# A transformer block's attention stage: the second head group's queries made between the first four heads, and the roots of the tiles' variances later in GpSimd's order

## The chip, the cores and the metric

The kernel runs on one core of a Trainium2 chip. The metric is the device time of one launch in microseconds; before the change it is 2590.26 us, the median of three runs (2590.1 to 2594.9).

The core has five engines with a queue each, which work through their queues in order: TensorE (PE in the profile; its weight loads are shown apart as PEld), VectorE (DVE), ScalarE (ACT), GpSimd (POOL) and SyncE (SP), which here only starts DMAs. GpSimd starts the gathers, DMAs whose rows are chosen by an index.

## The reference

Everything is fp32. `x` is 4 x 512 tokens of 512 features, `ctx` is 4 x 512 tokens of 256 features. Four branches are added to `x` one after the other, each on a layernorm of it:

```python
x = x + ssm(ctx, layernorm(x), ...)         # a selective scan
x = x + moe(layernorm(x), ...)              # 64 experts, 8 for each token, rerouted by similarity
x = x + attention(layernorm(x), ctx, ...)   # the stage that the change touches
x = x + ffn(layernorm(x), w1, w2)           # quantized, ternary weights

def attention(h, ctx, Wq, Wk, Wv, Wo, gq, gk):      # 16 heads of 128
    q = rmsnorm(h @ Wq, gq)                         # normed for each token and head
    k = rmsnorm(ctx @ Wk, gk)
    v = ctx @ Wv
    attn = softmax(q @ k.T / sqrt(128))             # for each batch and head, 512 x 512
    return (attn @ v) @ Wo
```

The layernorm in front needs, for each token, the mean and the variance of its 512 features and the variance's inverse root. The MoE branch ends with a weighted sum of eight rows for each token.

## The kernel before

The phases run one after the other: the scan, the routing, the experts, and then `attend` (L1808), which holds the attention and the FFN and takes about the second half of the time. In `attend` the order of instructions is the program's own: each engine's queue gets them in the order in which the Python code emits them, and no scheduler moves them.

Tokens come in tiles of 128: four tiles for each of four batches. Heads come in groups of four; a group is a batch with four heads, 16 groups in all, 64 heads. A head's work on one tile is a *unit*, so a head has four units and `u` counts them, 0 to 255.

The steps of a tile (batch 0 at the start, later batches while the batch before is at work):
- `fetch` (L1835): one gather by GpSimd of 128 rows of the experts' outputs (256 KB). Eight for each tile. They land in four buffers `yg` in turn, and in the first tiles in `yg_first` (four places) and `yg_more` (eight places) too.
- `add` (L1844): VectorE adds the weighted row to `x_all`.
- `stats` (L1850): on VectorE mean and variance (`bn_stats`, `bn_aggr`), and on GpSimd the addition of epsilon and the power -0.5 (L1857, L1859), which gives `rstd_c`.
- `normed` (L1862): VectorE makes `xn_c`, which waits for `rstd_c`.
- `turn_x` (L1868): four transposes on TensorE, and a copy to `xnT` by ScalarE.

The steps of the queries of a tile for a group:
- `queries` (L1910): four matmuls with 512 columns into `pq`; ScalarE squares them into `sq`.
- `norm_q` (L1921): VectorE sums the squares of each head (`qms`, L1924), GpSimd makes the inverse root `rq` (L1926, L1927).
- `scale_q` (L1930): VectorE multiplies, `qn`.
- `turn_q` (L1935): four transposes on TensorE into `pqt`, a copy to `qT` by ScalarE.

The steps of a unit: `scores` (L1945: a matmul, the maximum `mx` on VectorE, exp on ScalarE), `weights` (L1958, VectorE: reciprocal and scaling), `turn` (L1963: transposes `pet`, copy `eT` by ScalarE). Once a head, `values` (L1972) multiplies by v, after the last `eT` of its head is there. Once a head and group, `project` (L1980) multiplies by Wo for one tile of the group before.

Two parts of `attend` set the order:

*The first tiles.* A list of steps is made with `later(time, step)`, sorted by time (L2260), and emitted. The times have no effect but the order. It holds the 32 fetches and additions of batch 0 (L2191 to L2196), eight whole key tasks (`some_keys`: keys of later heads, `pk`, whose results SP stores to `k_dram`), and then for each of the four tiles one window (L2217 to L2239): `turn_x`, two more key tasks, the queries of groups 0 *and* 1, the scores of head 0 on this tile, and some of the weights and turns. Loads of Wq (1 MB each), of the keys, their norms and the values of head 0, 1 and 2 (`load_kv`) and the norming of those keys (`norm_k`, by VectorE here) have their times in the list too (L2240 to L2244). As SP works in order, a load whose turn has come behind a key's store starts when this store has been started.

*The loop over units* (L2270), from `u = 4` on: the scores of `u`, the values of the head before where `i == 2`, the turn of `u - 2`, then what `front[u]` holds (TensorE's extra work), the weights of `u - 1`, and what `back[u]` holds (work without TensorE). `front` and `back` are filled from L2101 on. For the groups 1 to 14 the loop makes the queries of the group behind: of each head `h` the tile `h`'s, at `u + 1` to `u + 4` (L2110 to L2115). In group 0's heads it makes none, as group 1's have been made between the first tiles. In the loop, keys are normed by GpSimd (L2123), and GpSimd fetches three rows of the next batch for each head (L2130).

Of the kernel before, what the change touches and what calls it, by code (L numbers as in the profile page):

```python
# [17 lines left out]
F32 = mybir.dt.float32  # L18
# [6 lines left out]
ALU = mybir.AluOpType  # L25
# [4 lines left out]
P = 128  # L30
B, S, DM = 4, 512, 512
NT = B * S // P
NC = DM // P
CTX = 256
EPS = 1e-5
DS, DC, DR = 16, 4, 16
NG = 4
E, TOPK, SEL, FI = 64, 8, 4, 192
# [692 lines left out]
def moe_phase(ctx, cm, x_all, w, kv, dr, router_stats, out):  # L731
# [33 lines left out]
    with tc.manual_schedule():  # L765
        attend(cm, x_all, w, kv, y_dram, r["wk"], r["pos"], tern, late, ctx_k, keys.wk, out)
# [386 lines left out]
class Keys:  # L1153
# [4 lines left out]
    KB = S // P  # L1158
# [649 lines left out]
def attend(ctx, cm, x_all, w, kv, y_dram, wk, pos, tern, late, ctx_k, wk_k, out):  # L1808
# [5 lines left out]
    tc, nc = cm.tc, cm.nc  # L1814
    pool = {n: ctx.enter_context(tc.tile_pool(name=f"c_p{n}", bufs=n)) for n in (1, 2, 3, 4, 7)}
    small = ctx.enter_context(tc.tile_pool(name="c_small", bufs=3))
# [5 lines left out]
    KB = S // P  # L1822
    NG4 = H // HG
    half = pool[1].tile([P, HG], F32, name="half")
    nc.vector.memset(half, -0.5)
    groups = [(b, g) for b in range(B) for g in range(NG4)]
    heads = [(b, g, h) for b, g in groups for h in range(HG)]
    xnTs, st = {}, {}
# [21 lines left out]
    def stats(t, name):  # L1850
# [8 lines left out]
        nc.gpsimd.tensor_tensor(rstd, ve, half[:, 0:1], ALU.pow)  # L1859
        st[name, t] = mv, rstd  # L1860

    def normed(t, name):  # L1862
        mv, rstd = st.pop((name, t))
        xn = st[name, t] = pool[1].tile([P, DM], F32, name=f"xn_{name}")
        nc.vector.tensor_scalar(xn, x_all[:, t, :], mv[:, 0:1], rstd, ALU.subtract, ALU.mult)
        return xn
# [154 lines left out]
    def ffn_x(t):  # L2021
        xn = normed(t, "d")
        mx = small.tile([P, 1], F32, name="mxa")
        nc.vector.tensor_reduce(mx, xn, AX.X, ALU.max, apply_absolute_value=True)
        ff[t] = scales(mx, tern.mean[0], "a")
# [75 lines left out]
    front, back = {}, {}  # L2101

    def put(where, u, f, *a):
        where.setdefault(u, []).append((f, *a))

    last = len(groups) - 1
    for n, (b, g, h) in enumerate(heads):
        j = n // HG
        u = n * KB
        if j < last and j > 0:  # L2110
            after = groups[j + 1]
            put(front, u + 1, queries, *after, h)
            put(back, u + 2, norm_q, *after)
            put(back, u + 3, scale_q, *after)
            put(front, u + 4, turn_q, *after, h)  # L2115
        if j > 0:
            put(front, u + 4, project, j - 1, h)
            put(back, u + 5, take_projected, j - 1, h)
        if h == 0:
            put(back, u, load_q, j + 2)  # L2120
            put(back, u + 1, load_o, b, g)
        put(back, u + 3, load_kv, n + 3)
        put(back, u + 3, norm_k, n + 2)  # L2123
        at = n % H
        if b + 1 < B:
            for k in range(3):
                if 0 <= 3 * (at - 2) + k < NC * TOPK:
                    put(back, u + k, add, 1)
            if 0 <= 3 * (at - 1) < NC * TOPK:
                put(back, u + 2, fetch, min(3, NC * TOPK - 3 * (at - 1)))  # L2130
            if at >= 11 and at < 15:
                t = (b + 1) * NC + at - 11
                put(back, u + 1, stats, t, "c")
                put(back, u + 3, normed, t, "c")
                put(front, u + 4, turn_x, t)
        if b > 0 and h == 1:
            t = (b - 1) * NC + g
            put(back, u + 2, stats, t, "d")
            put(back, u + 4, ffn_x, t)
            put(back, u + 5, ffn_xq, t)  # L2140
            put(front, u + 6, ffn_xT, t)

            put(front, u + 7, ffn_up, t, 0)
            put(front, u + 11, ffn_up, t, 1)
            for k, at in enumerate((8, 9, 12, 12)):
                put(back, u + at, ffn_max, t, k)
            put(back, u + 12, ffn_h, t)
            for k in range(4):
                put(back, u + 13 + k // 2, ffn_hq, t, k)
            put(front, u + 14, ffn_hT, t, 0)  # L2150
            put(front, u + 15, ffn_hT, t, 1)
            put(front, u + 15, ffn_down, t, 0)
            put(front, u + 19, ffn_down, t, 1)
            put(back, u + 20, ffn_y, t)
            put(back, u + 21, store, t)
# [26 lines left out]
    def later(time, f, *a):  # L2182
        steps.append((time, len(steps), f, a))

    START, GAP, FLIGHT = 3.0, 1.35, 6.0
    FRONT, WINDOW = 21.0, 14.5

    wide = [pool[1].tile([P, KB, S], F32, name="yg_first", tag="eT")]
    wide += [pool[2].tile([P, HG, DM], F32, name="yg_more", tag="Wo") for _ in range(2)]
    places = [t[:, k] for t in wide for k in range(KB)]  # L2190
    for n in range(NC * TOPK):  # L2191
        at = n % 16 - KB
        if n >= 16 and 0 <= at < KB:
            at = -1
        later(START + n * GAP, fetch, 1, places[at] if at >= 0 else None)
        later(START + n * GAP + FLIGHT, add, 1)  # L2196

    left = list(KEYS_LATE)

# [13 lines left out]

    for i in range(H // 2):
        later(2.6 * i, some_keys)
    later(FRONT + 0.4, key_ends)
    for i in range(NC):  # L2217
        end = START + ((i + 1) * TOPK - 1) * GAP + FLIGHT
        later(end + 0.1, stats, i, "c")
        later(end + 2.3, normed, i, "c")  # L2220
        at = FRONT + i * WINDOW
        later(at, turn_x, i)
        later(at + 0.5, key_task)
        later(at + 2.2, queries, 0, 0, i)
        later(at + 5.6, key_ends)
        later(at + 6.4, norm_q, 0, 0)
        later(at + 6.5, queries, 0, 1, i)
        later(at + 8.5, scale_q, 0, 0)
        later(at + 10, turn_q, 0, 0, i)
        later(at + 10.4, key_task)  # L2230
        later(at + 10.8, norm_q, 0, 1)
        later(at + 12.1, scores, 0, i)
        later(at + 12.9, scale_q, 0, 1)
        later(at + 13, key_ends)
        later(at + 14, turn_q, 0, 1, i)
        if i < KB - 1:
            later(at + 14.7, weights, 0, i)
        if i < KB - 2:
            later(at + 15, turn, 0, i)  # L2239
    for f, n, time in ((load_q, 0, 9.5), (load_kv, 0, 14.5), (load_q, 1, 17.5), (load_kv, 1, 44),  # L2240
                       (load_kv, 2, 50)):
        later(time, f, n)
    for n in range(3):
        later(FRONT + (0, 2.5, 3.2)[n] * WINDOW + 9, norm_k, n, nc.vector)  # L2244

    def last_norms():
        rsqrt(nc, small, ms, ms, "late")
# [22 lines left out]
    for u in range(KB, len(heads) * KB + 2):  # L2270
        n, i = divmod(u, KB)
# [30 lines left out]
    for i in range(NC + 1):  # L2302
        t = t0 + i
# [103 lines left out]
```

## Time and profile before

| | us |
|---|---|
| median of three runs | 2590.26 |
| the profiled execution, its own time | 2586.95 |
| its span in the trace | 2585.2 |
| TensorE busy | 2444.9 (95%) |
| VectorE busy | 1497.1 (58%) |
| ScalarE busy | 1210.4 (47%) |
| GpSimd busy | 1179.4 (46%) |
| granted TensorE clock, mean | 0.978 |

Stages of the trace, by TensorE's instructions:

| stage | from | to | TensorE busy, share | clock |
|---|---|---|---|---|
| scan, routing, experts | 0 | 1339.0 | 1239.28, 93% | 0.97 |
| eight key tasks, first gathers | 1339.0 | 1363.2 | 22.30, 92% | 0.91 |
| windows of the four first tiles | 1363.2 | 1436.1 | 66.83, 92% | 0.91 |
| units 4 to 16 | 1436.1 | 1468.6 | 28.92, 89% | 1.00 |
| units 17 to the last head | 1468.6 | 2506.0 | 1024.84, 99% | 1.00 |
| last tiles' FFN | 2506.0 | 2585.0 | 62.68, 79% | 0.98 |

How to read it: times count from the start of the span. In a line of the trace stand the start, the duration, the engine, the line of the program, the operation with its output and inputs, how many were merged, and in brackets how long the engine had stood idle before it and what released it. A PE row's duration ends when its last result is there; the next row can start before this, so the pace is read from start to start. The clock is the share of TensorE's full speed that was granted; 0.5 is half speed. An engine that is idle costs time only where something that sets the end waits for it.

### The profile page before, as it was taken

How to read it: one execution, taken by the hardware profiler on the slowest of the kernel's cores; microseconds unless marked ns; L12 is line 12 of the kernel's file. 1: busy time of each engine (PE TensorE's matmuls, PEld its weight loads, DVE VectorE, ACT ScalarE, POOL GpSimd, SP SyncE). 2: the span in 40 equal slices, each digit the busy share in tenths (PEclk: the TensorE clock that was granted, in tenths of full speed). 3: DMA queues.
4: the chain of work that ended last, by engine and by line, in shares of the span. 5: the costliest groups of instructions: out<-in, count | busy, mean ns of one | idle time of the engine just before them, and what ended most of it. 6: DMA issues, size and time to landing. Idle time of an engine off the chain costs nothing. (4 is left out here: it accounts for less than half of the span.)

```text
span 2585.2 us, 29327 instructions
## 1 busy us (share of the span) xinstructions
PE 2444.9 (95%) x9781; PEld 1377.1 (53%) x9831; DVE 1497.1 (58%) x2565; ACT 1210.4 (47%) x2323; POOL 1179.4 (46%) x1105
## 2 busy tenths in 40 slices
PE   6989889987999999999998999999999999999997
PEld 3555555645556566667664444445455554554543
DVE  6999998945322443344225565456655666555446
ACT  6777777654232222233323543454454454544543
POOL 7999999923333444444425333134322343121112
PEclk8999999988999999999998999999999999999999
DMA  5362535244666677899756543233433453332210
GB/s 203 95 224 88 202 126 190 101 141 166 197 211 215 215 227 251 278 336 336 251 172 196 182 122 112 82 112 109 132 104 100 138 143 102 96 95 64 62 48 21
DMA packets 228013, 403.60 MB, mean 156 GB/s; under 512 B 62211, under 2 KB 103235, under 8 KB 223760
## 3 DMA queue, kind: packets, MB, share of 16 engines
q1 hardware_dynamic: 184798, 246.71, 29.4%
q0 software_dynamic: 41008, 154.76, 19.2%
q8 instruction: 81, 1.33, 0.2%
q10 hardware_dynamic: 2050, 0.18, 0.1%
q14 instruction: 76, 0.62, 0.1%
HBM read 313.88 MB, written 79.82 MB: 152 GB/s over the span
## 5 line engine op out<-in xcount | busy, mean ns | idle before, releaser
L1952 DVE TENSOR_REDUCE mx<-psc 128x1 f32<-128x512 f32 x256 | 176.6, 690 | 403.1 <-PE psc L1949 402.9
L1282 PE MATMUL pg<-xT,wg 128*128 128x284 f32 (+12 forms) x1536 | 394.2, 400 | 1.8 <-ACT xT L1269 1.1
L1955 ACT ACTIVATE e<-psc,mx 128x512 f32<-128x512 f32 x256 | 176.1, 688 | 325.2 <-DVE mx L1952 324.6
L1282 PEld LDWEIGHTS pg<-xT,wg 128*128 128x128 f32 x1536 | 279.0, 192 | 85.4 <-issue 36.5
L492 POOL TENSOR_TENSOR dBu<-bb,du 128x1024 f32<-128x1024 f32 x128 | 304.6, 2400 | 4.0 <-DVE dA L517 2.8
L1223 POOL DMA_INDIRECT xg<-xn_dram,tok x168 | 173.9, 1035 | 198.7 <-PE pt L1266 156.3
L1949 PE MATMUL psc<-kT,qT 128*128 128x512 f32 x512 | 261.7, 593 | 0.0
L1976 PE MATMUL po<-eT,v 128*128 128x512 f32 x512 | 231.4, 595 | 8.5 <-ACT eT L1970 8.3
L1915 PE MATMUL pq<-Wq,xnT 128*128 128x512 f32 x512 | 231.7, 595 | 0.0
L1985 PE MATMUL px<-Wo,oT 128*128 128x512 f32 x512 | 231.5, 595 | 0.0
L1969 PEld LDWEIGHTS pet<-ident,e 128*128 128x128 f32 x1024 | 126.3, 141 | 147.3 <-issue 129.0
L1926 POOL TENSOR_SCALAR qms<-qms 128x4 f32<-128x4 f32 x64 | 24.9, 389 | 390.5 <-DVE qms L1924 389.6
L503 ACT ACTIVATE dA<-delta,negA 128x512 f32<-128x512 f32 x256 | 176.5, 695 | 49.3 <-DVE hc L518 27.1
L517 DVE TENSOR_TENSOR_SCAN dA<-dA,dBu 128x1024 f32<-128x1024 f32 x80 | 185.4, 2318 | 14.9 <-ACT dA L503 5.2
L1327 DVE COPY yo<-po 128x512 f32<-128x512 f32 x68 | 47.0, 691 | 217.4 <-PE po L1316 217.4
L1976 PEld LDWEIGHTS po<-eT,v 128*128 128x128 f32 x512 | 96.1, 190 | 134.7 <-issue 114.6
L1969 PE MATMUL pet<-ident,e 128*128 128x128 f32 x1024 | 154.8, 274 | 7.0 <-DVE e L1961 6.8
L523 PEld LDWEIGHTS yT<-ident,hc 128*128 128x128 f32 x1024 | 119.1, 144 | 78.7 <-issue 36.1
L1961 DVE TENSOR_SCALAR e<-e,tot 128x512 f32<-128x512 f32 x256 | 155.0, 605 | 9.1
L523 PE MATMUL yT<-ident,hc 128*128 128x128 f32 x1024 | 133.1, 278 | 20.5 <-POOL hc L518 9.0
L1223 POOL DMA_INDIRECT wd<-down,widx x64 | 62.8, 981 | 194.0 <-PE po L1316 181.6
L1970 ACT COPY eT<-pet 128x512 f32<-128x512 f32 x256 | 148.2, 579 | 3.4 <-PE pet L1969 2.9
(358 smaller groups left out, 4276.4 us busy)
## 6 DMA issues: line engine op xcount, KB each, us to landing
y_dram<-yo SPq DMA_DIRECT2D x110, 256.0 KB
bb<-bc_dram SPq DMA_DIRECT2D x16, 1024.0 KB
cb<-bc_dram SPq DMA_DIRECT2D x16, 1024.0 KB
v_dram<-v SPq DMA_DIRECT2D x64, 256.0 KB
k_dram<-k_kT SPq DMA_DIRECT2D x64, 256.0 KB
Wq<-Wq SPq DMA_DIRECT2D x16, 1024.0 KB
kT<-k_dram SPq DMA_DIRECT2D x64, 256.0 KB
rk<-r_dram SPq DMA_DIRECT2D x64, 256.0 KB
```

The source lines that it names most:

```text
L492: nc.gpsimd.tensor_tensor(dBus[q], st[b]["bb"][i // 2][:, j:j + 2, :], st[b]["du"][c].unsqueeze(1).to_broadcast([P, 2, S]), ALU.mult)
L503: nc.scalar.activation(dAs[q][:, j, :], st[b]["delta"][c], AF.Exp, scale=negA[:, c, n:n + 1])
L517: nc.vector.tensor_tensor_scan(*flat, 0.0, ALU.mult, ALU.add)
L523: nc.tensor.matmul(yT[:, lc, :], t[:, lc * P:(lc + 1) * P], cm.ident, is_transpose=True, start=first and lc == 0, stop=last, skip_group_ch ...
L1223: nc.gpsimd.indirect_dma_start(out=t[0:n, :], out_offset=None, in_=table, in_offset=bass.IndirectOffsetOnAxis(ap=index, axis=0))
L1282: nc.tensor.matmul(pg[:, 0:n], s["wg"][:, c, m * P:(m + 1) * P], s["xT"][:, c, 0:n], start=c == 0, stop=c == NC - 1)
L1915: nc.tensor.matmul(pq.rearrange("p h d -> p (h d)"), xnTs[b * NC + i][:, c, :], s["Wq"][:, c, :], start=c == 0, stop=c == NC - 1)
L1949: nc.tensor.matmul(pscore, st[b, g]["qT"][:, h, i * P:(i + 1) * P], ks[n], start=True, stop=True)
L1952: nc.vector.tensor_reduce(mx, pscore, AX.X, ALU.max, negate=True)
L1969: nc.tensor.transpose(pt[:, kc, :], e[:, kc * P:(kc + 1) * P], cm.ident)
L1976: nc.tensor.matmul(po, v[:, kc, :], eT[:, kc, :], start=kc == 0, stop=kc == KB - 1)
L1985: nc.tensor.matmul(px, oTs[j * HG + h][:, i * P:(i + 1) * P], st[b, g]["Wo"][:, h, :], start=h == 0, stop=h == HG - 1)
```

## The change

The queries of group 1 leave the windows of the first tiles. They go into the loop, to the units of the first four heads: of head `h` the queries at unit 4 + 3h, the sums and roots one unit later, the scaling two, the turn three units later.

In the first tiles, `stats` is split for them: `stats_c` has the VectorE part, `root_c` the two GpSimd instructions, which are put 2.2 later in the list, so behind more fetches in GpSimd's order.

The times of the list are set anew: a fetch every 1.27, from the 15th on every 1.56, additions 5.5 instead of 6.0 behind; the windows start at 20.6, 32, 44 and 56.5 instead of every 14.5 from 21 on. In a window the second key task stands where the second group's queries stood, the scores at 11.9 instead of 12.1. The loads move: the first Wq from 9.5 to 13.6, head 0's keys from 14.5 to 18.2, the second Wq from 17.5 to 45, heads 1 and 2's keys from 44 and 50 to 50 and 56.

```diff
+    def stats_c(t):
+        sts = small.tile([P, 6], F32, name="st_c")
+        nc.vector.bn_stats(sts, x_all[:, t, :])
+        mv = small.tile([P, 2], F32, name="mv_c")
+        nc.vector.bn_aggr(mv, sts)
+        st["c", t] = mv
+
+    def root_c(t):
+        mv = st["c", t]
+        ve = small.tile([P, 1], F32, name="ve_c")
+        nc.gpsimd.tensor_scalar(ve, mv[:, 1:2], EPS, None, ALU.add)
+        rstd = small.tile([P, 1], F32, name="rstd_c")
+        nc.gpsimd.tensor_tensor(rstd, ve, half[:, 0:1], ALU.pow)
+        st["c", t] = mv, rstd
...
-        if j < last and j > 0:
+        if j == 0:
+            at, after = KB + 3 * h, groups[1]
+            put(front, at, queries, *after, h)
+            put(back, at + 1, norm_q, *after)
+            put(back, at + 2, scale_q, *after)
+            put(front, at + 3, turn_q, *after, h)
+        elif j < last:
...
-    START, GAP, FLIGHT = 3.0, 1.35, 6.0
-    FRONT, WINDOW = 21.0, 14.5
+    FETCH = [3.4 + 1.27 * n + 0.29 * max(0, n - 14) for n in range(NC * TOPK)]
+    FLIGHT = 5.5
+    FRONT = (20.6, 32, 44, 56.5)
...
-        later(START + n * GAP, fetch, 1, places[at] if at >= 0 else None)
-        later(START + n * GAP + FLIGHT, add, 1)
+        later(FETCH[n], fetch, 1, places[at] if at >= 0 else None)
+        later(FETCH[n] + FLIGHT, add, 1)
...
-        end = START + ((i + 1) * TOPK - 1) * GAP + FLIGHT
-        later(end + 0.1, stats, i, "c")
+        end = FETCH[(i + 1) * TOPK - 1] + FLIGHT + 0.1
+        later(end, stats_c, i)
+        later(end + 2.2, root_c, i)
         later(end + 2.3, normed, i, "c")
-        at = FRONT + i * WINDOW
+        at = FRONT[i]
         later(at, turn_x, i)
         later(at + 0.5, key_task)
         later(at + 2.2, queries, 0, 0, i)
         later(at + 5.6, key_ends)
         later(at + 6.4, norm_q, 0, 0)
-        later(at + 6.5, queries, 0, 1, i)
+        later(at + 6.5, key_task)
         later(at + 8.5, scale_q, 0, 0)
-        later(at + 10, turn_q, 0, 0, i)
-        later(at + 10.4, key_task)
-        later(at + 10.8, norm_q, 0, 1)
-        later(at + 12.1, scores, 0, i)
-        later(at + 12.9, scale_q, 0, 1)
-        later(at + 13, key_ends)
-        later(at + 14, turn_q, 0, 1, i)
+        later(at + 8.9, key_ends)
+        later(at + 9.8, turn_q, 0, 0, i)
+        later(at + 11.9, scores, 0, i)
         if i < KB - 1:
-            later(at + 14.7, weights, 0, i)
+            later(at + 15.5, weights, 0, i)
         if i < KB - 2:
-            later(at + 15, turn, 0, i)
-    for f, n, time in ((load_q, 0, 9.5), (load_kv, 0, 14.5), (load_q, 1, 17.5), (load_kv, 1, 44),
-                       (load_kv, 2, 50)):
+            later(at + 16, turn, 0, i)
+    for f, n, time in ((load_q, 0, 13.6), (load_kv, 0, 18.2), (load_q, 1, 45), (load_kv, 1, 50),
+                       (load_kv, 2, 56)):
         later(time, f, n)
```

On GpSimd the order of the first tiles becomes: fetches 0 to 13, the root of tile 0, fetches 14 to 17, `norm_q` of tile 0, fetches 18 to 20, the root of tile 1, fetches 21 to 25, `norm_q` of tile 1, fetches 26 to 28, the root of tile 2, fetches 29 to 31, `norm_q` of tile 2, the root of tile 3, `norm_q` of tile 3. Before, it was: fetches 0 to 11, the root of tile 0, fetches 12 to 18, `norm_q` of tile 0 for group 0, fetch 19, the root of tile 1, fetches 20 and 21, `norm_q` for group 1, fetches 22 to 27, the root of tile 2, and so on.

More of the change, by code (lines that the diff above doesn't have):

```diff
@@ L2215, in attend @@
         later(2.6 * i, some_keys)
-    later(FRONT + 0.4, key_ends)
+    later(FRONT[0] + 0.45, key_ends)
     for i in range(NC):
-        end = START + ((i + 1) * TOPK - 1) * GAP + FLIGHT
-        later(end + 0.1, stats, i, "c")
+        end = FETCH[(i + 1) * TOPK - 1] + FLIGHT + 0.1
+        later(end, stats_c, i)
+        later(end + 2.2, root_c, i)
         later(end + 2.3, normed, i, "c")
-        at = FRONT + i * WINDOW
+        at = FRONT[i]
         later(at, turn_x, i)
@@ L2226, in attend @@
         later(at + 6.4, norm_q, 0, 0)
-        later(at + 6.5, queries, 0, 1, i)
+        later(at + 6.5, key_task)
         later(at + 8.5, scale_q, 0, 0)
-        later(at + 10, turn_q, 0, 0, i)
-        later(at + 10.4, key_task)
-        later(at + 10.8, norm_q, 0, 1)
-        later(at + 12.1, scores, 0, i)
-        later(at + 12.9, scale_q, 0, 1)
-        later(at + 13, key_ends)
-        later(at + 14, turn_q, 0, 1, i)
+        later(at + 8.9, key_ends)
+        later(at + 9.8, turn_q, 0, 0, i)
+        later(at + 11.9, scores, 0, i)
         if i < KB - 1:
-            later(at + 14.7, weights, 0, i)
+            later(at + 15.5, weights, 0, i)
         if i < KB - 2:
-            later(at + 15, turn, 0, i)
-    for f, n, time in ((load_q, 0, 9.5), (load_kv, 0, 14.5), (load_q, 1, 17.5), (load_kv, 1, 44),
-                       (load_kv, 2, 50)):
+            later(at + 16, turn, 0, i)
+    for f, n, time in ((load_q, 0, 13.6), (load_kv, 0, 18.2), (load_q, 1, 45), (load_kv, 1, 50),
+                       (load_kv, 2, 56)):
         later(time, f, n)
-    for n in range(3):
-        later(FRONT + (0, 2.5, 3.2)[n] * WINDOW + 9, norm_k, n, nc.vector)
+    for n, time in enumerate((29, 62, 66)):
+        later(time, norm_k, n, nc.vector)
     def last_norms():
```

## The prediction

> **What bounds the kernel.** I read the engines' shares first, then the granted clock and the engines' busy time stage by stage, then TensorE in order of time through the stretch that the change touches. TensorE (PE) carries the kernel: 2444.9 of 2585.2 us, and it makes 42% of the chain of waits against 3% for the next engine. But the share hides stages. The busy times of TensorE, cut at turn_x of the tiles 0 to 3 (1363.2, 1385.8, 1403.6, 1421.2), at the loop's first score (1436.1) and at its unit 17 (1468.6), are these (columns: stretch, its length, busy and instructions, clock, DMA share, GB/s):
>
> ```profile
> 1363.20:1385.80 22.60, 19.38 (x62) 0.82 0.67 230
> 1385.80:1403.60 17.80, 16.20 (x61) 0.94 0.73 216
> 1403.60:1421.20 17.60, 16.85 (x61) 0.90 0.25 81
> 1421.20:1436.10 14.90, 14.40 (x56) 1.00 0.09 33
> 1436.10:1468.60 32.50, 28.92 (x104) 1.00 0.69 217
> ```
>
> The last window, nothing waiting and the clock full, takes 14.9 us; the first three take 22.6, 17.8 and 17.6. So the first tiles hold 13.3 us of waits and half clock, the first four heads about 5. Nothing else in the kernel is touched, so the gain has to come from these. TensorE's own rows show where it goes:
>
> ```profile
> 1384.93 1.12 PE L1942 MATMUL pqt<-ident,qn 128*128 128x128 f32 x4 [3.06 <-DVE qn L1933]
> ...
> 1403.10 0.66 PE L1942 MATMUL pqt<-ident,qn 128*128 128x128 f32 x4 [1.50 <-DVE qn L1933]
> 1403.59 0.60 PE L1872 MATMUL pt<-ident,xn_c 128*128 128x128 f32 x4
> 1404.44 0.69 PE L1969 MATMUL pet<-ident,e 128*128 128x128 f32 x4 [0.25 <-ACT qT L1943]
> 1404.92 3.58 PE L1182 MATMUL pk<-k_ctx,k_w 128*128 128x512 f32 x4
> ...
> 1421.59 1.88 PE L1182 MATMUL pk<-k_ctx,k_w 128*128 128x512 f32 x4
> 1423.31 3.60 PE L1915 MATMUL pq<-Wq,xnT 128*128 128x512 f32 x8
> ```
>
> The reader is to see that a wait is paid twice: the pause itself (3.06, 1.50), and the same four key matmuls at 3.58 instead of 1.88 us behind it.
>
> **What moves out of the first tiles.** Start to start, at full clock: queries 3.43 us (1423.31 to 1426.74), its four turns 0.44. The second group's four of each leave: 4 x 3.87 = 15.5 us of TensorE. Their squares, sums, roots, scalings and copies leave with them; those lay beside TensorE. Of SP's queue, the second Wq (1 MB) goes from 1359.8 to behind the third tile's first key store, the first Wq behind two more key stores (1352.2 to about 1357), head 0's key and value loads behind the eighth store (1357.0 to about 1362). I cost these at nothing: the first Wq still has 10 us before its first use, where the trace shows 2.5 MB (Wq, Wo, a key, its norms) landing in the 12 us from 1435.0 to 1447.3. If that cover fails, the first window ends 2 to 3 us later. Below nothing is possible too: gathered rows land in 7.5 us beside the two Wq's and in 3.2 to 5.6 without.
>
> **What this leaves on the path.** Less TensorE work saves only where TensorE sets the pace, and after the change the windows are set by a ring of static orders. In GpSimd's new order the root of tile 1 stands behind norm_q of tile 0 and three fetches; that norm_q stands behind tile 0's queries. So from turn_x to turn_x, in rows of the trace:
>
> - Tile 0. Fetch 11 starts at 1356.94; two more at 1.26 end at 1360.4; the root takes 0.24 + 0.97, xn_c 0.6: turn_x at 1362.4 against 1363.20. In GpSimd's old order it stalled 3.38 us for this root; the new place removes that, as meant, but what it frees is fetches, not the end.
> - Window 0. turn_x to the end of queries as now (1363.20 to 1373.27) 10.1; end of queries to end of the root rq 3.0 (2.8 at 1426.91 to 1429.69, 3.7 in the first window); fetches 18 to 20 at 1.3 each 3.9; root 1.1 and xn_c 0.6: 18.7, so turn_x(1) at 1381.1 (now 1385.84). TensorE idles from about 1376.5.
> - Window 1. turn_x 0.44, score 0.86, keys 1.72, queries 3.60, and 3.0 more because 4.6 us of pause leave the first three at half clock: 9.6. Then 2.9 + 3.9 + 1.7: 18.1, turn_x(2) at 1399.2 (now 1403.59).
> - Window 2. 5.8 + 2.2 for half clock; rq 2.8; scaling 0.7, the last addition 0.7, statistics 0.9 (DVE's order has them behind the scaling); 1.7: 14.8, turn_x(3) at 1414.0 (now 1421.15).
> - Window 3. 5.8 + 1.1 (half of the half-clock price); rq 2.8, scaling 0.7, turns with their copy 1.3, score 0.9: 12.6, the loop at 1426.6 (now 1436.12).
>
> So the first tiles give back 9.5 us, not 15.5.
>
> The half clock is where a rule is weighed. The Trainium skill, TensorE: Matmul & The Clock Gate, section HAM oscillation, puts the danger at PE idle gaps over about 3.4 us; it speaks against this change, which turns a full TensorE into one with pauses of 4.6 and 3.9 us. The rows above are stricter: half clock behind 3.06 and behind 1.50 + 0.25. By the rule window 3 (pause 2.4) is at full clock, by the rows it pays 2.2; I took 1.1. Windows 1 and 2 pay by both.
>
> **What the heads pay.** Units 4 to 16 now take 32.5 us for 13 x 1.30 (score 0.86, turn 0.44) + 3 x 3.43 (values) = 27.2 us of work; 5.3 are waits, like this one:
>
> ```profile
> 1449.48 1.02 PE L1949 MATMUL psc<-kT,qT 128*128 128x512 f32 x2
> 1451.47 3.70 PE L1976 MATMUL po<-eT,v 128*128 128x512 f32 x8 [0.97 <-ACT eT L1970]
> ```
>
> Added are the 15.5 us. Could they fall into the 5.3? Only where they stand between a score and what waits for it. Queries go to units 4, 7, 10, 13, values are at 6, 10, 14. Behind unit 13's queries the wait of the values goes, and some 0.35s behind two short units go. But behind unit 7's: DVE's queue holds the sum qms (0.69) ahead of the ninth score's maximum, exp behind it is ahead of the copy eT on ScalarE, and this copy is what values wait for: end of queries, score 1.0, maximum, reciprocal and scaling 1.4, qms 0.7, maximum 0.6, exp 0.9, copy 0.6 make 5.2, while TensorE has only 3.5 to do: 1.8 us instead of 0.97. The scaling qn waits on DVE for GpSimd (2.1 from sum to qn at 1427.63 to 1429.72), with the next maximum queued behind it, worth some 0.5 once or twice. GpSimd's wait for head 3's norms (9.2 us, until 1447.3, 11.2 behind the loop's start) is over before unit 7's sum comes, some 18 behind the start, so it costs nothing. Gains and losses come out even, to +0.6: the heads pay 15.5 + 0.6 = 16.1, with ends of 11 (all waits filled) and 18 (a 1.8 us pause also brings half clock, 1.7).
>
> **The sum:** -9.5 + 16.1 = +6.6 us, as a difference of the profiled execution (span 2585.2, its own time 2586.95, 1.75 outside the span, unchanged). On the median 2590.26 this makes **2596.9, slower**. A measurement of this kernel can tell about 0.2% (5.2 us) from no change: the three runs themselves span 4.8.
>
> **Rivals.**
> - *TensorE stays at full clock (not slower).* It decides from the point where no window of the new front starts at half clock. Window 0 then takes 6.4 instead of 10.1 to its queries' end, windows 1, 2, 3 lose 3.0, 2.2, 1.1: the loop starts at 1416.6, the front gives 19.5, the sum is -3.4: 2586.9. For it: less work waits in TensorE's queue. Against it: the pauses that I find are longer than those which brought half clock. 0.2.
> - *The heads absorb.* All 5.3 us of waits filled, +10.2 to +11: with -9.5 about +1, 2591.5. For it: later heads, with two such fillers each, take 16.48 for 15.93 of work. Against: those have four times as much between score and values. 0.15.
> - *Both together:* -9, 2581. 0.08.
> - *Worse:* first Wq or head 0's norms late (+3), half clock in the heads (+1.7): 2601.5. 0.15.
> - My forecast, 2594 to 2599.5: 0.42.
>
> Slower by over 0.2% is the last two but a part of the forecast's lower end: 0.52. Within: the absorbing heads, most of the full-clock case and that end: 0.35. Faster: 0.13. The range leaves out "both" and the far end of "worse": 2585.5 to 2603.
>
> **What would show it.** Right: turn_x at about 1362, 1381, 1399 and 1414, TensorE idle 3 to 5 us before the second and third with xn_c as the releaser, the clock of these windows still under 0.95, GpSimd waiting 5 to 7 us for qms behind fetch 17; the loop some 9.5 us earlier; unit 17 some 6 us later than 1468.6, with a wait of about 2 us at the second po. Wrong: windows of 12 us, or units 4 to 16 in under 46 us. The stage behind unit 17 must be as long as now (1037.4 us to 2506.0); if it differs, the cause lies outside this account.

## The result, and the profile after

The changed kernel takes 2599.61 us (median of 11 runs, 2591.8 to 2605.48) against 2590.34 us of the kernel before in the same series (11 runs, 2581.79 to 2594.9): a ratio of 1.0037, with a 95% interval of 1.0026 to 1.0049. It is slower by 9.3 us; 6.6 were forecast. Its profiled execution took 2598.65 us, 11.7 more than that of before.

The head of its page, with the engines' busy time:

```profile
span 2596.9 us, 29375 instructions
...
PE 2452.8 (94%) x9831; PEld 1377.5 (53%) x9831; DVE 1493.6 (58%) x2565; ACT 1209.1 (47%) x2323; POOL 1177.2 (45%) x1105
```

No work was added or taken away, only moved. TensorE is busy 7.9 us longer, 4.5 of them in the windows and the first four heads, where its clock is lower, and idle 3.8 us longer. The stages, cut as for the kernel before, at turn_x of the tiles 0 to 3, at the loop's first score and at unit 17's (columns: stretch, its length, TensorE's busy time and instructions, granted clock, DMA share, GB/s):

```profile
1365.00:1382.30 17.30, 12.64 (x49) 0.84 0.76 269
1382.30:1400.00 17.70, 15.67 (x49) 0.79 0.48 139
1400.00:1415.10 15.10, 13.74 (x47) 0.84 0.76 245
1415.10:1429.40 14.30, 12.94 (x44) 0.86 0.34 104
1429.40:1478.10 48.70, 45.25 (x151) 0.98 0.41 122
```

The four windows now take 64.4 us instead of 72.9, though 15.5 us of TensorE's work have left them, and their clock is lower than before (0.79 to 0.86 against 0.82 to 1.00). Units 4 to 16 take 48.7 instead of 32.5. So 8.5 us are won and 16.2 are lost. TensorE's rows in the windows show why so little is won:

```profile
1377.96 0.64 PE L1957 MATMUL pqt<-ident,qn 128*128 128x128 f32 x4
1382.27 1.12 PE L1887 MATMUL pt<-ident,xn_c 128*128 128x128 f32 x4 [3.68 <-DVE xn_c L1880]
...
1384.89 2.96 PE L1182 MATMUL pk<-k_ctx,k_w 128*128 128x512 f32 x4
...
1395.02 1.05 PE L1202 MATMUL kpss<-ones,k_sq 128*128 128x1 f32 x8 [0.69 <-ACT k_sq L1191]
...
1397.24 2.06 PE L1964 MATMUL psc<-kT,qT 128*128 128x512 f32 x2 [0.68 <-ACT qT L1958]
1399.96 1.12 PE L1887 MATMUL pt<-ident,xn_c 128*128 128x128 f32 x4 [0.66 <-DVE xn_c L1880]
1400.87 3.50 PE L1182 MATMUL pk<-k_ctx,k_w 128*128 128x512 f32 x4
...
1427.68 3.50 PE L1964 MATMUL psc<-kT,qT 128*128 128x512 f32 x4 [0.68 <-ACT qT L1958]
```

The reader is to see one long pause before the second turn_x, then small ones: in every window for the squares of the key task that took the place of the second group's queries (0.69, in the first window 0.75), and in the last three for the copy `qT` ahead of the score (0.68). Behind them the same four key matmuls take 2.96 and 3.50 us instead of 1.96, and two scores 3.50. GpSimd, in the same stretch, shows the chain that ends the first window:

```profile
1368.77 0.95 POOL L1839 DMA_INDIRECT yg<-y_dram,pos  x1 [0.30 <-issue]
1375.13 0.63 POOL L1941 TENSOR_SCALAR qms<-qms 128x4 f32<-128x4 f32 x1 [5.41 <-DVE qms L1939]
1375.84 1.04 POOL L1942 TENSOR_TENSOR rq<-qms,half 128x4 f32<-128x4 f32 x1
1377.07 1.09 POOL L1839 DMA_INDIRECT yg<-y_dram,pos  x1 [0.18 <-issue]
1378.47 0.96 POOL L1839 DMA_INDIRECT yg<-y_dram,pos  x1 [0.30 <-issue]
1379.73 0.94 POOL L1839 DMA_INDIRECT yg<-y_dram,pos  x1 [0.31 <-issue]
1380.71 0.27 POOL L1872 TENSOR_SCALAR ve_c<-mv_c 128x1 f32<-128x1 f32 x1
1381.06 0.58 POOL L1874 TENSOR_TENSOR rstd_c<-ve_c,half 128x1 f32<-128x1 f32 x1
```

Behind fetch 17 GpSimd stands 5.41 us for the sum `qms` of tile 0's queries; then come `rq`, three fetches, the root of tile 1, and TensorE's turn_x at 1382.27. In the heads, the rows that mattered:

```profile
1438.16 3.70 PE L1991 MATMUL po<-eT,v 128*128 128x512 f32 x8 [0.77 <-ACT eT L1985]
...
1443.87 3.60 PE L1930 MATMUL pq<-Wq,xnT 128*128 128x512 f32 x8
...
1452.84 3.70 PE L1991 MATMUL po<-eT,v 128*128 128x512 f32 x8 [1.56 <-ACT eT L1985]
...
1465.90 0.63 PE L1957 MATMUL pqt<-ident,qn 128*128 128x128 f32 x4 [0.31 <-DVE qn L1948]
```

The values of the second head wait 1.56 us behind unit 7's queries, longer than any did before (0.97), and those of the first 0.77 instead of 0.42; those of the third and fourth have no wait left.

### The profile page after: what moved, and what is told of

Its sections match the earlier page's. It is cut to its first block, busy times and chain, and to the rows that moved or that the text cites. A ratio compares the mean times of both kernels' runs of the same rounds, so it can differ in the third digit from the quotient of the medians.

```text
span 2596.9 us, 29375 instructions
## 1 busy us (share of the span) xinstructions
PE 2452.8 (94%) x9831; PEld 1377.5 (53%) x9831; DVE 1493.6 (58%) x2565; ACT 1209.1 (47%) x2323; POOL 1177.2 (45%) x1105
## 5 line engine op out<-in xcount | busy, mean ns | idle before, releaser
L523 PEld LDWEIGHTS yT<-ident,hc 128*128 128x128 f32 x1024 | 117.6, 142 | 80.9 <-issue 40.4
```

Of the source, the lines that this page charges most:

```text
L523: nc.tensor.matmul(yT[:, lc, :], t[:, lc * P:(lc + 1) * P], cm.ident, is_transpose=True, start=first and lc == 0, stop=last, skip_group_ch ...
```

## The experiments

All were profiled and timed. For each profile I cut the front in three, in us: **A**, from the first key matmul of `attend` to the first turn_x; **B**, from there to the maximum of the loop's first score; **C**, from there to the values of the fourth head. One profile is one execution; the ratio comes from all runs.

| kernel | A | B | C | B + C | A + B + C | ratio to before, 95% |
|---|---|---|---|---|---|---|
| before | 24.1 | 74.0 | 37.9 | 111.9 | 136.0 | |
| e9_before (the same) | 26.4 | 73.0 | 37.8 | 110.8 | 137.2 | 1.0010 [0.9997, 1.0024] |
| after | 22.9 | 66.2 | 53.7 | 119.9 | 142.8 | 1.0037 [1.0026, 1.0049] |
| e8_again (after) | 33.3 | 64.1 | 53.6 | 117.7 | 151.0 | 1.0045 [1.0026, 1.0064] |
| e1_queries | 27.8 | 75.0 | 53.5 | 128.5 | 156.3 | 1.0084 [1.0060, 1.0108] |
| e2_rest | 23.4 | 81.6 | 37.9 | 119.5 | 142.9 | 1.0040 [1.0020, 1.0060] |
| e2b_rest | 31.2 | 76.8 | 37.8 | 114.6 | 145.8 | 1.0022 [1.0006, 1.0039] |
| e3_root | 27.3 | 64.5 | 53.8 | 118.3 | 145.6 | 1.0037 [1.0022, 1.0053] |
| e4_one | 31.5 | 64.6 | 49.7 | 114.3 | 145.8 | 1.0036 [1.0021, 1.0051] |
| e6_places | 23.5 | 69.5 | 50.9 | 120.4 | 143.9 | 1.0066 [1.0045, 1.0088] |
| e7_three | 29.3 | 67.6 | 40.4 | 108.0 | 137.3 | 1.0001 [0.9981, 1.0020] |
| e10_both | 22.7 | 68.6 | 41.4 | 110.0 | 132.7 | 0.9987 [0.9974, 0.9999] |
| e11_fill | 32.2 | 60.6 | 53.5 | 114.1 | 146.3 | 1.0048 [1.0030, 1.0065] |
| e12_ends | 31.2 | 71.5 | 41.0 | 112.5 | 143.7 | 1.0000 [0.9986, 1.0013] |

C repeats to 0.3 us where the same work stands in the heads. A does not: in the changed kernel it is 22.9 and 33.3. A difference of a few us in B or C is therefore read from the stage, and a ratio tells it only where it is larger than its interval.

**The queries alone (e1_queries).** Only the move into the loop, with before's list of times, windows and loads.

```diff
-        later(at + 6.5, queries, 0, 1, i)
-        later(at + 10.8, norm_q, 0, 1)
-        later(at + 12.9, scale_q, 0, 1)
-        later(at + 14, turn_q, 0, 1, i)
...
+        if j == 0:
+            at, after = KB + 3 * h, groups[1]
+            put(front, at, queries, *after, h)
```

> Only the second group's queries move into the first four heads; list of times, loads and roots stay as before. All stages are counted from the first key matmul of the attention stage (before: the loop's first score at 97.0, unit 17 at 129.5; after: 87.3 and 136.0). Theory (the ring of GpSimd's order sets the windows, the heads pay for the moved work in full): loop's start at 84 to 88, units 4 to 16 in 48 to 49.5 instead of 32.5, in all 4 to 7 us slower than before. Rival (the new times and the later roots cost the time, the moved queries do not): loop's start at 82 or earlier, no slower than before.

Slower by about 21 us where 4 to 7 were expected, a miss by 14. The heads pay their 15.6 (C), but B gives back nothing at all: 75.0. All of TensorE's waits of over 0.5 us between the first turn_x and the loop:

```profile
1380.65 1.12 PE L1942 MATMUL pqt<-ident,qn 128*128 128x128 f32 x4 [3.70 <-DVE qn L1933]
1389.49 1.05 PE L1969 MATMUL pet<-ident,e 128*128 128x128 f32 x4 [1.64 <-DVE e L1961]
1401.37 1.11 PE L1942 MATMUL pqt<-ident,qn 128*128 128x128 f32 x4 [3.63 <-DVE qn L1933]
1410.09 1.09 PE L1969 MATMUL pet<-ident,e 128*128 128x128 f32 x4 [1.64 <-DVE e L1961]
1421.09 1.12 PE L1942 MATMUL pqt<-ident,qn 128*128 128x128 f32 x4 [2.79 <-DVE qn L1933]
1437.28 1.10 PE L1942 MATMUL pqt<-ident,qn 128*128 128x128 f32 x4 [2.79 <-DVE qn L1933]
```

The second group's queries had stood between the first group's queries and their turn. They were the cover of the chain of sum, root and scaling. Without them, and with the second key task still behind the turn, TensorE stands 2.8 to 3.7 us in every window, and what follows runs at half clock (0.75 to 0.89 in the windows). In the changed kernel the second key task stands ahead of the turn, in their place. No run moves that task alone, so that it is what makes the move bearable is argued here and not shown.

**The rest alone (e2_rest, e2b_rest).** Fetch times, split statistics, later loads; the queries and the windows as before. The second Wq at 21 in the list, then again at 17.5.

```diff
-    for f, n, time in ((load_q, 0, 9.5), (load_kv, 0, 14.5), (load_q, 1, 17.5), (load_kv, 1, 44),
+    for f, n, time in ((load_q, 0, 13.6), (load_kv, 0, 18.2), (load_q, 1, 21), (load_kv, 1, 50),
```

> Only the rest of the change: fetch and addition times, roots later in GpSimd's order, first Wq and the keys' loads later (the second Wq 3.5 later in the list only, as its queries stay in the windows). Theory: TensorE is full in these windows, so the loop starts within 2 us of before's 97.0, units 4 to 16 take 32.5, the total is the same as before within 2.5 us. Rival (the new times carry the loss): loop's start 3 us or more later than 97.0.

> As the run of the rest alone, but the second Wq is loaded right behind the seventh key store, ahead of head 0's keys, so that the queries of both groups have their weights. Theory (TensorE is full in these windows, so the later roots bring nothing and cost nothing): the 5.2 us wait for Wq is gone, loop's start within 3 us of before's 97.0 (first key matmul = 0), the fourth po within 3 us of 136.0, total within 3 us of before. Rival (the later roots or additions cost time by themselves): the fourth po 4 us or more later than before.

In e2_rest the second group's first queries wait 5.18 us for their Wq, which is part of its 1.0040. Without this wait e2b_rest is still 0.2% slower than before, with B + C 2.7 to 3.8 us longer, between the two cases of the expectation, and waits of 4.43 and 3.04 us for `qn` in the first two windows. The fetches and roots set anew help nothing while the second queries are there. The parts do not add up: the queries alone cost some 21 us, the rest alone some 6 (by the ratio), together 9. The new window order and the second Wq's later load are in neither of the two; by this difference they take back most of it.

**The root's place (e3_root).** The root directly behind the statistics in the list, so behind one fetch instead of three after `norm_q`.

```diff
-        later(end + 2.2, root_c, i)
+        later(end, root_c, i)
```

> The changed kernel, with the roots put right behind the statistics in the list: one fetch instead of three stands between norm_q of a tile and the root of the next. Theory (the ring sets the windows): turn_x of tile 1 comes 2 to 3 us earlier than in the changed kernel (40.2 there), that of tile 2 3 to 5 earlier (57.8 there), the loop's start at 82.5 to 85 instead of 87.3; the heads take 48.7 as there; 2 to 5 us faster than the changed kernel. Rival (half clock and TensorE's work set the windows): loop's start within 1 us of 87.3.

TensorE's pause before the second turn_x falls from 3.68 us to 1.29, and the third turn_x comes 16.0 us behind the second instead of 17.7. The last window but one gives part of it back (16.0 instead of 15.1). The time is after's, where 2 to 5 us less were expected. What is late next is seen on VectorE ahead of the fourth turn_x:

```profile
1412.71 0.69 DVE L1948 TENSOR_TENSOR qn<-pq,rq 128x512 f32<-128x512 f32 x1 [0.26 <-POOL rq L1942]
1415.83 0.75 DVE L1847 SCALAR_TENSOR_TENSOR x_all<-yg_more,wk,x_all 128x512 f32<-128x512 f32 x1 [2.43 <-DMA yg_more<-y_dram,pos]
1416.62 0.69 DVE L1864 BATCH_NORM_STATS2 st_c<-x_all 128x6 f32<-128x512 f32 x1
```

The last gathered row of the tile lands after everything else is done, and statistics, root and turn_x follow it. So the place of the root is worth 1 to 2 us in a window, and rows that are still on the way take part of them back. In the whole of B nothing is left of it: 64.5, and 66.2 and 64.1 in the two profiles of after.

**Tiles put back (e4_one, e7_three).** For the first tile, or the first three, the second group's queries stand again in front of the next tile's turn_x, where TensorE pauses; in e7_three the fourth tile's are at unit 9. In both the second Wq, which is needed early again, is loaded at 22 in the list instead of 45.

```diff
+        if i < 3:                                # 1 in e4_one
+            then = FETCH[(i + 2) * TOPK - 1] + FLIGHT + 0.1
+            later(at + 9.85, queries, 0, 1, i)
+            later(then + 2.35, norm_q, 0, 1)
+            later(then + 5, scale_q, 0, 1)
+            later(FRONT[i + 1] + 5.65, turn_q, 0, 1, i)
```

> The changed kernel, with the second group's queries of tile 0 put back, into TensorE's 3.7 us pause ahead of turn_x of tile 1; their root comes behind tile 1's root in GpSimd's order. Theory (the pause is free time of a ring that GpSimd sets, and the half clock behind it costs 2 us more): turn_x of tile 1 stays within 1 us (17.3 behind that of tile 0), its window gets no longer, from the loop's start to the fourth po 3.5 to 4.5 us less than the changed kernel's 53.7; in all 3.5 to 6 us faster than the changed kernel. Rival (each query costs its 3.9 us wherever it stands): the same as the changed kernel within 1.5 us.

> As the run with one tile put back, but with tiles 0, 1 and 2 put back, each ahead of the next tile's turn_x, and tile 3's queries at unit 9, right ahead of head 1's values. Theory (ring of 15 to 18 us per window, TensorE's work 10.7 of it): the loop starts 0 to 4 us later than in the changed kernel, the heads to the fourth po take 41 to 42.5 instead of 53.7; the fourth po 127 to 135, so 1 to 9 us faster than before. Rival (what goes back makes the windows as long as before): loop's start at 97 or later, no faster than before.

C falls by 4.0 for one tile and by 13.3 for three: 4.0 and 4.4 a tile, what the prediction's 3.87 of TensorE work for a tile and its waits say. B, 64.1 and 66.2 in the two profiles of after, is 64.6 and 67.6: in the windows the queries stand in a pause and are nearly free. With three tiles put back the kernel is as fast as before (1 to 9 us faster was expected), and B + C is 2.8 and 3.9 us shorter than in before's two profiles. In e4_one 3.5 to 6 us less than after were expected, and the 4 us of C do not show in the ratio.

**Other units (e6_places).** The loop's queries at units 5, 9, 13 and 16 instead of 4, 7, 10 and 13, so that each stands directly ahead of a score and the values.

```diff
-            at, after = KB + 3 * h, groups[1]
+            at, after = (5, 9, 13, 16)[h], groups[1]
+            soon = h == HG - 1                   # its norm, scaling and turn a unit closer
```

> The changed kernel, with the second group's queries at units 5, 9, 13 and 16 instead of 4, 7, 10 and 13, so that they stand right ahead of each head's values. Theory (the moved queries leave the waits ahead of values, 0.77 at the first and 1.56 at the second po, because they stand at the wrong units): these waits go, and the fourth po comes 1.5 to 3 us earlier than in the changed kernel (142.8 there, 136.0 before), so still 3.5 to 5.5 later than before. Rival (only TensorE's work counts, or DVE's order makes new waits of the same size): the fourth po within 1 us of 142.8.

The waits at the values go (C is 2.8 lower), but the head behind pays them back: it takes 19.7 us instead of 16.8, since unit 17's own queries, for the group after, stand 4.73 us behind those of unit 16. The time is not better than after's (1.0066, 4 runs).

**The changed kernel again (e8_again).**

> The changed kernel once more, to see how far one execution's front differs from another's. Theory: from the loop's start to the fourth po 53.7 within 0.5; the time from turn_x of tile 0 to the loop's start between 64 and 70; the time to turn_x of tile 0 22 to 28, by how late the gathers and key stores land. Rival (the first trace is typical): all within 1 us of it.

B and C repeat to 2.1 and 0.1 us, A does not, and neither does the time (2604.18, ratio 1.0045). What held A up is in the section on what was not expected.

**Before again, and TensorE's pauses filled (e9_before, e11_fill).** The first is the kernel before without an edit. The second adds eight matmuls to the changed kernel whose result is not used: four before the second turn_x, one before the third, one each between turn and score in the last three windows (the expectation's "six" and "seven" are miscounts).

```diff
+        if i:
+            later(at + 11.8, fill, 1, i)
         later(at + 11.9, scores, 0, i)
+        if i < 2:
+            later(FRONT[i + 1] - 0.02, fill, (4, 1)[i], i)
```

> The kernel before once more, for a second profile of it. Both theories expect a ratio of 1.000. They differ in where the front starts. In before's one profile the first turn_x stood 24.1 us behind attend's first key matmul; in seven profiles of variants it stood 22.9 to 33.3 behind it. Theory A (this spread is the execution's, since the code up to there does the same work): this profile shows any value from 23 to 33, and from the first turn_x to the fourth head's values 112 us as in the first profile. Theory B (the later loads of the change make the start late): 24 to 25 again.

> The changed kernel with six more matmuls whose result nobody reads: four in TensorE's pause before the second turn_x, one before the third, one in each of the windows 1 to 3 between the turn of the queries and the score (seven in all). The rival of the full clock: without pauses the windows 1 to 3 run at full clock, the half-clock price in after's trace (keys of the windows 1 to 3 at 2.96, 3.50 and 2.79 and the last score at 3.50 instead of 1.88: 1.1 + 1.6 + 0.9 + 1.6 = 5.2 us) goes, less some 1 us that the added matmuls take where the pause is shorter: from the second turn_x to the loop's first score 4 us less than after's 49.1, and the time 4 us under after's. My account (the chain through GpSimd sets the windows' ends, half clock only lengthens the way to the end of queries): the same 4 us, as every window's chain begins at the end of the queries; a rule of gaps over 3.4 us: only window 1 changes, 1.1 us.

The second profile of before has A at 26.4, nearer to theory B's 24 to 25 than to most variants, but two profiles cannot tell. The windows of e11_fill, cut as above:

```profile
1371.90:1390.40 18.50, 17.52 (x58) 0.82 0.44 134
1390.40:1405.70 15.30, 13.94 (x53) 1.00 0.56 157
1405.70:1419.10 13.40, 12.44 (x49) 1.00 0.85 284
1419.10:1431.30 12.20, 11.51 (x44) 1.00 0.25 81
```

With useless work in most of the pauses the clock is full in all of the last three windows, and they take 40.9 us instead of 47.1 (46.7 in e8_again), although four of the eight matmuls stand in them. Units 4 to 16 take 47.9. So half clock costs some 6.2 us in these windows, and the pauses of after have to do with it: 3.68 us once, and 0.66 to 0.69 two or three times in each window. All three windows are shorter, by 2.4, 1.7 and 2.1 us; a rule of gaps over 3.4 us has only the first of them gain. But not every pause was filled (the 0.69 for the squares stand in each window at full clock), and the pauses alone do not settle it. The last score of the windows and the loop's first, in e7_three and in e10_both, behind the same two waits of 0.69 and 0.67:

```profile
1437.10 3.45 PE L1964 MATMUL psc<-kT,qT 128*128 128x512 f32 x4 [0.67 <-ACT qT L1958]
...
1434.32 1.98 PE L1964 MATMUL psc<-kT,qT 128*128 128x512 f32 x4 [0.67 <-ACT qT L1958]
```

The first pair runs at half clock, the second at full. The time does not show the gain, though 4 us under after's were expected (1.0048): in this profile A is 32.2, 9.3 longer than in after's. Whether the fillers have a part in that is open.

**Both together (e10_both, e12_ends).** e10_both is e7_three with the root's place of e3_root. e12_ends moves also the column sums of the second key task behind the turn of the queries.

```diff
-        later(at + 8.9, key_ends)
+        later(at + 9.82, key_ends)
```

> Three tiles' second queries back between the first tiles (e7_three, 1.0001 of before) and the roots right behind the statistics (the order of e3_root). If the wait for the root ends the windows here too: windows 1 to 2 us shorter in all, ratio 0.9993 to 1.000 of before. If TensorE sets the windows, since its pauses are filled by the queries that were put back: the same as e7_three.

> e10_both with the end of the second key task (its column sums on TensorE, kpss) behind the turn of the queries instead of ahead of it. In e10_both's trace TensorE waits 0.69 to 0.75 us for ScalarE's k_sq ahead of the second kpss in each of the four windows, and 0.67 for the copy qT ahead of the last score; in the new order the turn fills the first wait and the kpss the second. If TensorE sets these windows: 0.5 to 0.7 less in each and another 0.7 in the last, 2 to 3 us in all, a ratio to before of 0.997 to 0.998. If the chain through GpSimd (queries, norms, root, next turn) sets them: nothing, 0.9987 as e10_both.

e10_both is the fastest, 2586.75 us (12 runs): well under the changed kernel, and at the edge of what can be told from before. It took a further 3.23 us of waits for loads in its first window (2.34 at the first queries, put down to the head's keys by the trace, 0.89 for the second Wq). What the root's place adds is not seen in the stage: the last three windows take 47.2 us in e7_three and in e10_both, and no turn_x behind the first waits for its root in e10_both. In e12_ends the waits of 0.7 us went and others came:

```profile
1384.48 0.66 PE L1957 MATMUL pqt<-ident,qn 128*128 128x128 f32 x4 [1.59 <-DVE qn L1948]
...
1403.56 0.63 PE L1957 MATMUL pqt<-ident,qn 128*128 128x128 f32 x4 [2.51 <-DVE qn L1948]
...
1421.12 0.63 PE L1957 MATMUL pqt<-ident,qn 128*128 128x128 f32 x4 [1.50 <-DVE qn L1948]
```

The turn now waits itself for `qn`, which the kpss had covered. So the chain of sum, root and scaling sets the pace inside the window, and the ratio is 1.0000, where 0.997 to 0.998 was the case of a TensorE that sets it.

## Why the prediction was right

- **The front.** From the first turn_x to the loop 64.2 us were forecast (1362.4 to 1426.6) and 64.4 measured, 62.2 in e8_again. Window by window it was 18.7, 18.1, 14.8 and 12.6 against 17.3, 17.7, 15.1 and 14.3. The first was sized too long by its first half (8.7 us to the end of the queries for 10.1: only the first key task ran at half clock). The last was too short by its second half: 7.1 us to the end of the queries for 6.9, but 7.2 from there to the loop for 5.7. The column sums of the second key task, 0.69 late for its squares, hold up the turn by 0.7, and the score takes 1.7 at half clock instead of 0.9. (The last window of before, read as free of waits, has one of 0.50 us for `qn`; nothing in the sum hangs on it.)
- **The pauses.** 4.6, 3.9 and 2.4 us were forecast before the three turn_x; they are 3.68, 0.66 and none. The ring of GpSimd's order holds as forecast for the first window (the wait for `qms` 5.41, three fetches, root, 1382.3 for 1381.1). In the second TensorE arrives late itself, at half clock, so the ring and TensorE end it nearly together; in the third no wait for `xn_c` is left. The new small waits behind the second key task were not in the account. So in the last two windows the half clock came without the pauses that it was forecast from. That the sizes fit there (7.8 us to the end of the queries for 8.0, and 7.1 for 6.9) is in part luck.
- **Half clock.** Here a rule stood against rows, and both were too simple. The Trainium skill, TensorE: Matmul & The Clock Gate, section HAM oscillation, speaks of gaps over about 3.4 us. By it the last two windows of after, which have no gap over 0.7 us, would take about 13.4 and 12.2 us, as with the pauses filled; they take 15.1 and 14.3. The page's next section, A second HAM failure mode, tells of a clock that falls because TensorE idles briefly but often between groups of matmuls; this fits after's windows, and e11_fill, where the clock is full once those gaps are fewer. The rows of before, read as "a pause of 1.5 us brings half clock", fail too: in e4_one a pause of 2.24 us was followed by keys at full speed (1.88), in e2b_rest one of 3.04. What brings it, by how many pauses in how long a stretch, stays open.
- **The heads.** 16.1 us were forecast, 16.2 measured (48.7 for 32.5), and C repeats it in all five profiles with the queries at these units (15.6 to 15.9 over before's 37.8 and 37.9). The wait at the second values is 1.56 for the 1.8 forecast, and 0.77 stands at the first. e4_one and e7_three show that the price goes with the tiles.
- **The later loads.** Cost at nothing, with 2 to 3 us if the cover fails: in after's trace the first queries wait 0.24 us for a DMA, in e10_both and e12_ends, where the second Wq is loaded early again, 2.34 and 2.80. The cover is thin, and the end that was named is what it costs there.
- **The rest.** The stage behind unit 17, from its score to the last unit's, is 1038.3 us for 1037.4. The profiled difference of 11.7 is made of 7.7 from the first turn_x to unit 17 (7.4 forecast), 0.9 in this stage, 1.3 behind it, and 1.8 because the first turn_x came at 1365.0 and not at 1363.2. It had been forecast 0.8 earlier; before it, `attend` itself began 3.0 later than in before's profile, with the same code ahead of it.
- **The rivals.** "Full clock" had the right price, 6.3 us for the last three windows (6.2 in e11_fill), but does not come by itself. "The heads absorb" is out: e6_places filled the waits of the values and paid in the next head. "Worse" (2601.5) is near e8_again's median of 2604.18, but neither of its two causes is what e8_again shows.

The forecast of 2596.9 lies 2.7 us under the measured median, just outside the interval of the ratio (6.7 to 12.7 us). The heads' term is confirmed, and the ring for the first window; the sum of the front came out right though two of its pauses and some of its waits did not. What the remaining 2.7 us are is not settled. In the profiles B + C is 5.8 to 9.1 us longer in after's two than in before's two, so 6.6 lies within their scatter. A later front is not supported: A is 22.7 to 33.3 us, on average 28.2, in the nine profiles of after and the variants made from it, and 24.1 and 26.4 in before's, but also 27.8 in e1_queries, whose code up to the first turn_x is before's. And over all fourteen profiles the ratio goes with B + C (correlation 0.89) better than with A + B + C (0.84), and hardly with A (0.10).

## What to carry to other kernels

Work that is taken out of a stage pays only by what TensorE did on the path of that stage. Where a chain through other engines ends each step, the removed work was its cover, and the emptied engine stands still; here it ran at a lower clock as well. Ask of each block first which wait it covers; moved to a stage that is nearly full (here 89%), it cost its whole length.

## What the runs showed that was not expected

The stretch before the first turn_x, eight key tasks beside the first gathers with the DMA engines busy for most of the time (0.79 in before, 0.77 in after), takes 23 to 33 us with the same work. In e8_again ScalarE and TensorE stood there:

```profile
1364.63 0.17 ACT L1214 ACTIVATE k_ms<-kpss 128x4 f32<-128x4 f32 x1 [6.63 <-remote]
```

ScalarE waits 6.63 us on a small copy of the key task, released by something that the trace does not name, and TensorE stands 5.56 us behind it and comes back at half clock (four key matmuls 3.76). In after's own profile no such wait is there; in e11_fill it is 2.71 and 2.43 us, in e9_before 2.76. In each of the eight profiles with A over 27 TensorE stands 2.1 to 6.4 us at once behind such a wait, and the next four key matmuls take 3.4 to 3.8 us; in the six with A under 27 it stands at most 1.4 there. So this wait makes most of the spread, and e1_queries shows that it comes with before's order too (4.21). What releases it is open: a store or a buffer on the busy DMA queues would fit, but that was not tried. The second profile of before shows the same kind of scatter elsewhere: TensorE waits 3.29 us for the second Wq, which had landed in time in the first profile.
